# Four-row strips, later turned values, and a last layer with paced loads, finer stores and a 64-row channel product

## The chip, the cores and the metric

The kernel runs on one core of a Trainium2 chip. A core has five engines that run side by side, each with its own instruction queue: TensorE (PE, matrix products, with weight loads listed apart as PEld), VectorE (DVE), ScalarE (ACT), GpSimd (POOL) and SyncE (SP), which only hands out transfers (DMAs). Engines wait for each other through semaphores; an instruction that waits holds up everything behind it in its own queue. Transfers between the large memory (DRAM) and the on-chip memory (SBUF) can be handed out by SP, ACT and POOL. Matrix products land in a small memory, PSUM, from which ACT or DVE copies them to SBUF.

The metric is device microseconds of the launch, as the median of several executions. A further execution is recorded by the profiler; its span runs from the first to the last instruction seen.

## The reference

Input is one image x of 48 channels and 256 x 256 pixels in fp32. Two layers follow, each added to its input, each on a group-normalised input (16 groups of 3 channels, over all pixels).

```
x = x + L0(gn(x));   x = x + L1(gn(x))

L0: qkv = depthwise3x3(w_qkv @ x)            # 144 channels: q, k, v
    cut q, k, v into 4x4 patches, 8 heads     # 66 x 66 patches, border ones are zero; 96 values per patch and head
    q, k scaled to unit length per patch
    attn = softmax(q.T k * temperature)       # per head
    out = v attn, patches put back, then w_proj @ out
L1: windows of 64 x 64 pixels:
    out[C,H,W] = sum over t<3, w, h, c of  x[c,h,w] Ws[t,w,W] Hs[t,h,H] Cs[t,c,C]
```

Within the image there are 4096 patches, so each head has a 4096 x 4096 matrix of logits. The zero border patches are brought in as one extra term of the softmax sum.

## The kernel before

**Stages.** First x is read, its group statistics are formed, and the 1x1 product of heads 0 and 1 is written to the DRAM tensor `t1[0]`. `depthwise_first` then makes q, k and v of head 0 (`qkv[0]` in DRAM). After that the attention loop runs over 8 heads `h` and 16 iterations `g` per head. Then comes the output projection with the second statistics (L783 to L862), and last the window layer (L866 to L1021).

**Attention loop.** One iteration g handles 256 patches of one head as two blocks of 128. Per block TensorE makes the logits (L344) into PSUM tiles `big`, three buffers of two banks, and ACT takes the exponential (L580) with the row sums; DVE scales the value block by them (L598). Then TensorE weighs the values (L614, three pairs per iteration), and DVE adds them up (L628). The order on every engine is the written one (`manual_schedule`). Into this loop is woven the work for the next head: the depthwise convolution of row r = g (loads L209, taps L232 on DVE, `patches`, `high`, `low`, stores L302), the loads of next keys, queries and values (`load_key`, `load_query`, `load_value`, all L318, nearly all from SP), and `turn` (L559), which transposes a value block with TensorE (L562) and copies it to `vT` with ACT (L564). `values[h, m]` is used by iterations g = 2m and 2m+1. `vt`, the block as loaded, has two buffers; `vT` has nine. For head 0, block g+1 is loaded at the top of iteration g (g = 1 to 6) and turned in the same iteration, behind the logits and ahead of the weighing. For later heads two blocks are loaded and turned in each of the iterations 11 to 14 of the head before.

**Strips.** The 1x1 product of heads 2 to 7 is too large to make ahead. It is made in strips of two rows from each half of the image, `class Strip` (L166): `load` brings x (L175, SP, two transfers), `run` makes two products into one `big` tile (L181) and ACT writes them with a bias to an `ot` buffer (L184), `store` writes to `t1[1]` (L193, SP, two transfers). Each iteration has four slots, k = 0 to 3, numbered through by s. Odd slots run two strips and then load the next two; even slots store the two of the slot before. There are 64 strips, so they fill the 64 slots of head 0. `xs` has three buffers of two rows, and `ots` three.

**Last layer.** Units are (yw, xh): one row of windows and half of its columns, 8 in all. `over_c` multiplies by Cs: for each image row one product over the channels (L923), rows of two window halves side by side in the array (partitions 0 to 48 and 64 to 112: 48 channels and a row of ones that carries the mean), into `pa`, three or two rows at a time; DVE or ACT copies it to `lzt` (L935, L933). `over_w` multiplies by Ws (L949) and ACT copies to `lyt` (L956); `over_h` multiplies by Hs (L968) and `residual` adds the input rows `lrt` (L982) and stores from POOL (L989). The opening `over_c(0)` runs alone; after that TensorE's order is, for each of three q of a unit, three times `over_w`, with two groups of the next unit's `over_c` behind each of the first two and `over_h` of the q before behind the third. `begin_load` takes one waiting transfer from a list (rows `lrt`, L884, or pieces `lxq`, L776) and issues it from ACT, where it stands in line with ACT's copies:

```
def begin_load():
    if loads:
        loads.pop(0)()
```

For the first three rows of windows the store waits for both halves and writes 8 channels at full width.

**Between the layers**, `occupy` (L840) puts filler products on TensorE: seven on a constant tile behind the last projection, and one behind each small product of the statistics.

Of the kernel before, what the change touches and what calls it, by code (L numbers as in the profile page):

```python
# [17 lines left out]
C = 48  # L18
# [21 lines left out]
NOT = 3  # L40
# [6 lines left out]
def conv_preact_kernel(  # L47
# [118 lines left out]
    class Strip:  # L166
# [5 lines left out]
        def load(self):  # L172
            self.xs = cv.tile([64 + C, 2, W], F32, name="xs", bufs=3)
            for s, rows in enumerate(both_halves(xc, 2 * self.j, 2)):
                nc.sync.dma_start(out=self.xs[s * 64 : s * 64 + C], in_=rows)  # L175

        def run(self, ps):
            self.ot = ots[self.j % len(ots)]
            for s in range(2):
                r = slice(s * 64, s * 64 + C)  # L180
                nc.tensor.matmul(  # L181
                    ps[:M1, s, :], lhsT=wr[r], rhs=self.xs[r].rearrange("p a b -> p (a b)"), start=True, stop=True
                )
            nc.scalar.activation(  # L184
                self.ot[:, :, 1 : W + 1],
                ps[:M1].rearrange("p s (a b) -> p (s a) b", a=2),
                AF.Identity,
                bias=bias[:M1, 1:2],
            )

        def store(self):
            for s, rows in enumerate(both_halves(t1[1], 2 * self.j, 2, base=1)):
                nc.sync.dma_start(out=rows, in_=self.ot[:, 2 * s : 2 * s + 2, :])  # L193
# [301 lines left out]

    ots = [cv.tile([M1, 4, W + 2], F32, name=f"ot{i}") for i in range(NOT)]
    for t in ots:
        nc.gpsimd.memset(t[:, :, 0:1], 0.0)
        nc.gpsimd.memset(t[:, :, W + 1 : W + 2], 0.0)
    depthwise_first()  # L500

    with tc.If(nc.values_load(large) > 0):
        with tc.tile_pool(name="sps", bufs=2, space=PSUM) as sps:
            for j in range(HALF // 2):
                w = Strip(j)
                w.load()
                w.run(sps.tile([128, 2, 512], F32, name="sps"))
                w.store()
# [27 lines left out]
    with tc.tile_pool(name="ahead", bufs=2) as ah, tc.tile_pool(name="ae", bufs=3) as ae, tc.tile_pool(  # L536
# [3 lines left out]
        NS = 3  # L540
        RP = TP // PX * KS
# [17 lines left out]
        def turn(h, m):  # L559
# [3 lines left out]
            vT = ah.tile([128, 4, HD], F32, name="vT", bufs=9)  # L563
# [89 lines left out]
        strips = [[Strip(s)] if s < HALF // 2 else [] for s in range(NH * NG * NK + 2)]  # L653
        for s in range(2):
            for w in strips[s]:
                w.load()
        with tc.manual_schedule():
            load_query(0, 1)
            block = scores(0, 0)
            for h in range(NH):  # L660
                more = h + 1 < NH
                rows = {r: Depthwise(h + 1, r) for r in range(CR + 1)} if more else {}
                for g in range(NG):
# [7 lines left out]
                    if h == 0 and 0 < g <= 6:  # L671
                        load_value(0, g + 1)
                    if more and CR + 2 <= g < CR + 6:
                        for m in range(2):
                            load_value(h + 1, (g - CR - 2) * 2 + m)
                    if more and CR + 3 <= g < CR + 6:
# [32 lines left out]
                    if h == 0 and 0 < g <= 6:  # L709
                        turn(0, g + 1)  # L710
                    if more and CR + 2 <= g < CR + 6:
                        for m in range(2):
                            turn(h + 1, (g - CR - 2) * 2 + m)
                    if p:
# [7 lines left out]
                    for k in range(NK):  # L722
# [10 lines left out]
                        if s % 2:  # L733
                            for w in strips[s - 1] + strips[s]:
                                w.run(big.tile([128, 2, 512], F32, name="big"))
                            for w in strips[s + 1] + strips[s + 2]:
                                w.load()
                        elif s:
                            for w in strips[s - 2] + strips[s - 1]:
                                w.store()  # L740
# [22 lines left out]
    CK = C + 1  # L763
    units = [(yw, xh) for yw in range(H // WS) for xh in range(2)]
    pieces = [lx.tile([64 + CK, PR, W], F32, name=f"lxq{i}") for i in range(NPC + 1)]
# [12 lines left out]
    with tc.tile_pool(name="pj", bufs=3) as pj, tc.tile_pool(name="pjs", bufs=1) as pjs, tc.tile_pool(  # L778
# [45 lines left out]
        csn = l1c.tile([64 + CK, T3 * C], F32, name="csn")  # L824
# [15 lines left out]
        def occupy(n):  # L840

            for _ in range(n):
                nc.tensor.matmul(busy[:, 0:2, :], lhsT=ident[:, :P2], rhs=nmx, start=True, stop=True)

        with tc.manual_schedule(engines={mybir.EngineType.PE}):
            occupy(7)
            mv1, e1 = group_stats(st1, mean1, rstd1, pjs, pp1, lambda: occupy(1))
            pc1 = pp1.tile([64 + CK, 1], F32, name="pc1", tag="pstat")
            nc.tensor.matmul(pc1, lhsT=gm2, rhs=e1, start=True, stop=True)
            occupy(1)  # L850
# [5 lines left out]
            nc.vector.tensor_scalar_mul(csn, csn, rstd2)  # L856
# [4 lines left out]
            occupy(1)  # L861
            nc.vector.tensor_sub(csn, csn, pb1)  # L862
# [3 lines left out]
    with tc.tile_pool(name="lz", bufs=2) as lz, tc.tile_pool(name="lr", bufs=6) as lr, tc.tile_pool(name="ly", bufs=2) as ly, tc.tile_pool(name="ps1", bufs=2, space=PSUM) as ps1, tc.tile_pool(  # L866
# [22 lines left out]
        loads = []  # L889

        def rows_later(yw, q):

            if yw < H // WS:
                for s in range(2):
                    for c in (0, 4):
                        loads.append(lambda s=s, c=c: load_rows(yw, q, s, c, 4, nc.scalar))

        def piece_later(n):

            yw, i = divmod(n, NPC)  # L900
            if yw < H // WS:
                for s in range(2):
                    for y in range(0, PR, PR // 2):
                        loads.append(lambda s=s, y=y: load_piece(yw, i, s, y, PR // 2, nc.scalar))

        def begin_load():

            if loads:
                loads.pop(0)()

        def over_c(u):
# [4 lines left out]
            for p in range(NPC):  # L916
                xq = piece(yw, p)
                for g, (y0, n) in enumerate(((0, 3), (3, 3), (6, 2))):
                    pa = ps1.tile([128, 2, 512], F32, name="pa")
                    for i in range(n):  # L920
                        for s in range(2):
                            r = slice(s * 64, s * 64 + CK)
# [9 lines left out]
                    if (p * 3 + g) % (4 if u else 2) == 1:  # L932
                        nc.scalar.copy(to, src)  # L933
                    else:
                        nc.vector.tensor_copy(to, src)  # L935
                    if xh and g == 2:
                        piece_later(yw * NPC + p + len(pieces))
                    yield
# [38 lines left out]
        def residual(u, q, pc):  # L977
# [5 lines left out]
            if yw < H // WS - 1:  # L983
                if xh == 0:
                    return
                cols = slice(0, W)
            for s in range(2):
                c0 = s * 24 + q * 8
# [74 lines left out]
```

## Time and profile before

| what | us |
|---|---|
| median of 3 runs | 3606.6 (3599.4 to 3610.64) |
| profiled execution | 3602.95 |
| its span | 3601.1 |
| TensorE busy | 3365.5 (93%) |
| DVE busy | 2026.6 (56%) |
| ACT busy | 1911.9 (53%) |
| POOL busy | 523.9 (15%) |
| first logits of head 0 in a row | from 284.3 |
| last weighing of head 7 | to about 3183 |
| projection and second statistics | to about 3337 |
| last layer | to 3594.5, last store after it |

A row of instructions names line, engine and operation, then out <- in with shapes, the count, busy time and mean duration in ns, and last the idle time before them with what ended it. fp32 matmuls appear as two records each. "A <- B: total, times, longest" is a wait of A that B ended. The granted clock is 1.00 at full speed. In 40 equal slices of the span TensorE is 90% busy or more from slice 17 to slice 35, and less in the slices before, around head 0, and after.

### The profile page before, as it was taken

How to read it: one execution, taken by the hardware profiler on the slowest of the kernel's cores; microseconds unless marked ns; L12 is line 12 of the kernel's file. 1: busy time of each engine (PE TensorE's matmuls, PEld its weight loads, DVE VectorE, ACT ScalarE, POOL GpSimd, SP SyncE). 2: the span in 40 equal slices, each digit the busy share in tenths (PEclk: the TensorE clock that was granted, in tenths of full speed). 3: DMA queues.
4: the chain of work that ended last, by engine and by line, in shares of the span. 5: the costliest groups of instructions: out<-in, count | busy, mean ns of one | idle time of the engine just before them, and what ended most of it. 6: DMA issues, size and time to landing. Idle time of an engine off the chain costs nothing.

```text
span 3601.1 us, 63050 instructions
## 1 busy us (share of the span) xinstructions
PE 3365.5 (93%) x25842; PEld 1871.5 (52%) x25842; DVE 2026.6 (56%) x2983; ACT 1911.9 (53%) x2890; POOL 523.9 (15%) x584
## 2 busy tenths in 40 slices
PE   2878898999999999999999999999999999976898
PEld 1334444555555555555555555555555555532675
DVE  5463665148825882587268727862885222258454
ACT  0245666557655665576456646764666444410443
POOL 2030111012211220122012211221121100010001
PEclk9999999999999999999999999999999999986899
DMA  7455655543332333233333323332233221059664
GB/s 156 165 114 158 156 156 143 166 129 92 87 86 84 97 81 89 83 92 86 82 86 97 91 80 83 94 90 81 80 96 93 64 57 37 19 121 289 140 158 108
DMA packets 240271, 384.10 MB, mean 107 GB/s; under 512 B 77618, under 2 KB 175266, under 8 KB 235464
## 3 DMA queue, kind: packets, MB, share of 16 engines
q1 hardware_dynamic: 187974, 244.77, 24.3%
q0 software_dynamic: 33728, 106.40, 13.1%
q10 hardware_dynamic: 18274, 28.83, 3.6%
q8 instruction: 206, 3.38, 0.4%
q14 instruction: 89, 0.73, 0.1%
HBM read 234.76 MB, written 144.90 MB: 105 GB/s over the span
## 4 chain that ended last, share of the span: by engine, by line
PE 81%; DMA 6%; DVE 2%; issue 1%; ACT 1%; SPq 1%; ACTq 0%; POOL 0%; POOLq 0%; DVEq 0%
PE big L344 38%; PE big L614 36%; PE pc L968 2%; PE pa L923 2%; PE pb L949 2%; DMA t<-ot 1%; PE big L181 1%; DMA pot<-os__70 1%; DMA vt<-qkv 1%; DMA lxq<-x1s 1%; DVE lzt L935 1%; DMA pad<-t 1%; PE pst L562 1%; DVE xt L810 1%; DMA x1s<-pxt 0%
## 5 line engine op out<-in xcount | busy, mean ns | idle before, releaser
L580 ACT ACTIVATE e<-big,nmx 128x1024 f32<-128x1024 f32 x1024 | 1144.3, 1118 | 902.8 <-PE big L344 886.9
L344 PE MATMUL big<-kt,qt 128*128 128x512 f32 x6144 | 1460.2, 395 | 35.1 <-DMA kt<-qkv 26.8
L614 PE MATMUL big<-e,vn 128*32 128x512 f32 x12288 | 1353.7, 595 | 1.0 <-DVE vn L598 1.0
L344 PEld LDWEIGHTS big<-kt,qt 128*128 128x128 f32 x6144 | 1142.6, 189 | 377.4 <-issue 120.1
L628 DVE TENSOR_TENSOR oacc<-big,oacc 128x1024 f32<-128x1024 f32 x359 | 438.6, 1222 | 784.2 <-PE big L614 784.2
L614 PEld LDWEIGHTS big<-e,vn 128*32 128x32 f32 x12288 | 385.2, 110 | 888.3 <-issue 818.1
L232 DVE SCALAR_TENSOR_TENSOR acc<-pad,dwt,acc 126x1024 f32<-126x1024 f32 x592 | 765.6, 1293 | 33.8 <-DMA pad<-t 13.4
L302 POOL DMA_DIRECT2D qkv<-o x72 | 53.1, 737 | 1349.0 <-ACT o L286 1349.0
L296 POOL TENSOR_TENSOR ol<-o,oh 126x1024 fp32r<-126x1024 f32 x78 | 185.2, 2375 | 277.3 <-DVE ss L247 204.4
L594 DVE TENSOR_REDUCE zt<-zs 128x1 f32<-128x5 f32 x256 | 38.7, 151 | 329.8 <-ACT e L580 329.8
L580 ACT ACTIVATION_READ_ACCUMULATOR e<-big,nmx 128x1 f32 x1024 | 196.4, 192 | 0.0
L286 ACT COPY o<-acc 126x1024 f32<-126x1024 f32 x74 | 160.7, 2172 | 0.0
L184 ACT ACTIVATE ot<-big,bias 108x1024 f32<-108x1024 f32 x64 | 68.9, 1112 | 136.7 <-PE big L181 71.0
L935 DVE COPY lzt<-pa 128x864 f32<-128x864 f32 (+1 forms) x69 | 102.1, 1525 | 63.5 <-PE pa L923 63.5
L956 ACT COPY lyt<-pb 128x1024 f32<-128x1024 f32 x69 | 70.9, 1028 | 112.6 <-PE pb L949 106.3
L803 PE MATMUL pps<-pot,wp 96*96 96x512 f32 x128 | 77.8, 773 | 53.3 <-DMA pot<-os__70 40.2
L213 ACT ACTIVATE acc<-pad,dwt 126x1024 f32<-126x1024 f32 x74 | 84.0, 1135 | 73.5 <-DMA pad<-t 73.5
L221 PE MATMUL dps<-pad,diag 126*126 126x512 f32 x216 | 96.4, 606 | 15.0 <-DMA pad<-t 15.0
L243 ACT ACTIVATE sq<-acc 126x1024 f32<-126x1024 f32 x74 | 78.4, 1060 | 59.8 <-DVE acc L232 48.9
L147 ACT ACT_TABLE_LOAD x2 | 2.6, 1283 | 202.6 <-DMA x1s<-pxt 149.2
L247 DVE TENSOR_REDUCE ss<-sq 126x64 f32<-126x1024 f32 x80 | 97.4, 1218 | 6.7 <-ACT sq L243 6.7
L949 PE MATMUL pb<-wsb,lzt 64*64 64x64 f32 x4608 | 88.8, 223 | 11.4 <-issue 7.2
(138 smaller groups left out, 1901.2 us busy)
## 6 DMA issues: line engine op xcount, KB each, us to landing
pad<-t SPq DMA_DIRECT2D x238, 254.0 KB
t<-ot SPq DMA_DIRECT2D x128, 217.7 KB
qkv<-ol POOLq DMA_DIRECT2D x78, 336.0 KB, 6.4
qkv<-oh POOLq DMA_DIRECT2D x70, 336.0 KB, 5.6
qt<-qkv SPq DMA_DIRECT2D x176, 96.0 KB
xs<-in_x_dram SPq DMA_DIRECT2D x128, 96.0 KB
pot<-os__70 SPq DMA_DIRECT2D x16, 768.0 KB
qkv<-o POOLq DMA_DIRECT2D x72, 168.0 KB, 3.4
```

Source lines behind the costliest of these rows:

```text
L213: nc.scalar.mul(self.acc, self.pad[:, 0:KS, 0:W], dwt[:, self.h, 0:1])
L221: nc.tensor.matmul(ps[:, i, :], lhsT=diag[:, tap, :], rhs=self.pad[:, y : y + 2, dx : dx + W], start=(tap == 0), stop=(tap == 8),)
L232: nc.vector.scalar_tensor_tensor(self.acc, self.pad[:, dy : dy + KS, dx : dx + W], dwt[:, self.h, tap : tap + 1], self.acc, ALU.mult, ALU.add,
L247: nc.vector.tensor_reduce(self.ss, self.sq.rearrange("p a (x b) -> p x a b", b=KS), AX.XY, ALU.add)
L286: nc.scalar.copy(self.o.rearrange("p (a b) x -> p a b x", a=KS), self.acc.rearrange("p a (x b) -> p a b x", b=KS))
L296: eng.tensor_sub(self.ol, self.o, self.oh.bitcast(F32))
L344: nc.tensor.matmul(ps[:, i, :], lhsT=qt[:, r, q0 : q0 + 128], rhs=kts[2 * j + i][:, r // 2, :], start=(r == 0), stop=(r == 2),)
L580: nc.scalar.activation(e[:, j * 1024 : (j + 1) * 1024], ps.rearrange("p a b -> p (a b)"), AF.Exp, bias=nmx[:, b : b + 1], accum_out=zs[:, ...
L614: nc.tensor.matmul(ps[p * 32 : (p + 1) * 32, u, :], lhsT=vn[:, c * 32 : (c + 1) * 32], rhs=e[:, n * 512 : (n + 1) * 512], start=(i == 0), ...
L628: nc.vector.tensor_add(oaccs[h, pair], ps, old)
L935: nc.vector.tensor_copy(to, src)
L949: nc.tensor.matmul(pb[s * WS : (s + 1) * WS, w, n * WS : (n + 1) * WS], lhsT=zts[u][r, t * C + b * 24 + q * 8 + s * 4 + i, :], rhs=wsb[r, ...
```

## The change

The edits lie in the attention loop, between the layers and in the last layer.

- **Strips** have four rows (`SR`), so there are 32; each has one load and one store per half. `run` makes two `big` tiles in turn. `xs` and `ots` have two buffers each. An odd slot runs one strip and loads the next; an even slot stores the strip of the slot before.
- **Values.** Head 0's blocks 2 to 7 are loaded at g = 1, 2, 4, 5, 7, 8 (`LOADS`) and each is turned two iterations later. For later heads block 7 is loaded at g = 1 of its own head and turned at g = 2. `vT` has eight buffers.
- **Channel product** over 64 partitions per half (`CF`) instead of 49: the weights of the added rows are zero, the pieces hold ones there.
- **Copies out of `pa`** run over the same elements with rows innermost instead of channels.
- **Loads of the last layer** are issued from SP, each behind a four-byte transfer to a DRAM scratch, `turns`, that reads one element of the tile just copied.
- **Stores of the last layer** come after each half: four of 4 channels and 128 columns.
- **Fillers** ahead of the statistics: two products on rows of the last projected tile and two on the statistics, instead of seven on a constant.

```
-            self.xs = cv.tile([64 + C, 2, W], F32, name="xs", bufs=3)
+            self.xs = cv.tile([64 + C, SR, W], F32, name="xs", bufs=2)
...
+            for i in range(0, SR, 2):
+                ps = pool.tile([128, 2, 512], F32, name="big")
...
-                    if h == 0 and 0 < g <= 6:
-                        load_value(0, g + 1)
+                    if h == 0 and g in LOADS:
+                        load_value(0, 2 + LOADS.index(g))
...
+                    if h > 0 and g == 1:
+                        load_value(h, NM - 1)
...
-                    if h == 0 and 0 < g <= 6:
-                        turn(0, g + 1)
+                    if h == 0 and g - 2 in LOADS:
+                        turn(0, 2 + LOADS.index(g - 2))
...
+                    if h > 0 and g == 2:
+                        turn(h, NM - 1)
...
-                        if s % 2:
-                            for w in strips[s - 1] + strips[s]:
-                                w.run(big.tile([128, 2, 512], F32, name="big"))
-                            for w in strips[s + 1] + strips[s + 2]:
-                                w.load()
+                        if s % 2 and s // 2 < len(strips):
+                            strips[s // 2].run(big)
+                            if s // 2 + 1 < len(strips):
+                                strips[s // 2 + 1].load()
+                        elif s % 2 == 0 and 0 < s // 2 <= len(strips):
+                            strips[s // 2 - 1].store()
...
-            occupy(7)
+            for ki in range(0, KS, 2):
+                occupy(xt[:, ys.start + ki : ys.stop : KS, :])
+            for i in range(0, 4, 2):
+                occupy(st1[:, : HALF * W // 512 - 3 + i, :])
...
-        def begin_load():
-
-            if loads:
+        def begin_load(behind):
+
+            if loads and behind is not None:
+                n = len(taken)
+                taken.append(nc.sync.dma_start(out=turns[:, n : n + 1], in_=behind))
                 loads.pop(0)()
...
-                            r = slice(s * 64, s * 64 + CK)
+                            r = slice(s * 64, s * 64 + CF)
...
+                    copy(to.rearrange("p s y k -> p s k y"), src.rearrange("p s y k -> p s k y"))
...
-                    yield
+                    yield zt[0:1, 0, y : y + 1]
...
-            for s in range(2):
-                c0 = s * 24 + q * 8
-                nc.gpsimd.dma_start(
-                    out=oc[c0 : c0 + 8, yw * WS : (yw + 1) * WS, cols].rearrange("c y x -> y c x"),
+            for c in (0, 4):
+                for s in range(2):
+                    c0 = s * 24 + q * 8 + c
+                    nc.gpsimd.dma_start(
+                        out=oc[c0 : c0 + 4, yw * WS : (yw + 1) * WS, cols].rearrange("c y x -> y c x"),
```

## The prediction

> **What bounds the kernel now.** I read the page's slices and chain first, then compared stretches of one head, then the waits and the chain of the slow head, then the last layer by clock and by shape.
>
> The first answer gives, for each stretch, its length, then busy time and instruction count of PE, PE's weight loads, DVE, ACT and POOL, the granted clock, the DMA share and GB/s. The first two lines are the last layer's opening channel product and the rest of that layer, the third is the head that also runs the strips, the fourth a later head.
>
> ```profile
> 3337.20:3359.30 22.10, 18.39 (x128) 15.62 (x128) 8.72 (x6) 8.71 (x6) 0.00 (x0) 0.50 0.31 57
> 3359.30:3594.50 235.20, 214.71 (x6080) 161.15 (x6080) 126.41 (x90) 100.36 (x90) 19.55 (x28) 0.98 0.60 140
> ...
> 330.80:739.90 409.10, 380.33 (x2316) 196.02 (x2320) 205.61 (x320) 253.19 (x361) 52.58 (x44) 0.95 0.58 156
> 760.00:1109.00 349.00, 349.00 (x2353) 195.74 (x2352) 221.62 (x344) 214.41 (x335) 59.75 (x56) 1.00 0.35 90
> ```
>
> The later heads have no idle TensorE at all, so nothing there can be won except work that is removed, and the change removes none. Head 0 has idle time, and so has the last layer. The chain of head 0, in order of time (start, length, what):
>
> ```profile
> 398.70 12.76 DMA t<-ot
> 411.46 0.02 issue
> 411.48 5.96 DMA vt<-qkv
> 417.44 0.04 issue
> 417.48 0.78 PE pst L562 x4
> 418.27 8.43 PE big L614 x64
> ```
>
> An iteration g that waits for nothing takes 25.74 us in head 0 (weighing starts at 512.12 and 537.86), 25.49 without the norm's matmul, plus 0.33 per turned block. From the weighing of g=1 (330.80) to that of g=15 (739.88) this makes 10 x 25.74 + 4 x 25.49 + 13 x 0.33 = 363.7; it took 409.1. **45 us are stall.** The waits of 330 to 760 us (total, times, longest) name three causes, which add up to 43.7:
>
> ```profile
> ACT ot L184 <- DMA t<-ot: 20.5, 7, 5.2
> ...
> PE pst L562 <- DMA vt<-qkv: 11.6, 5, 4.3
> ...
> PE big L181 <- DMA xs<-in_x_dram: 11.6, 3, 10.8
> ```
>
> All three transfers are handed out by one sequencer, SyncE, and in SyncE's own waits of this window "L175 <- PE big L181" stands with 52.8 us in 19 waits: it sits before a strip load until TensorE has read the buffer, with all later loads behind it.
>
> **The strips.** 64 strips of two rows become 32 of four; matmuls and activations keep number and shape. Loads and stores fall from 128 each to 64 each. At their median issue times (0.422 us for L175, 0.373 for L193) SyncE is spared 64 x 0.795 = 51 us, 3.2 per iteration; bytes are equal. What counts is lead. Before, a strip's buffer is that of three strips ago, whose store is issued one slot (a quarter iteration, 6.4 us) earlier, and the chain shows stores of 8.5 to 12.8 us. After, it is stored three slots (19 us) earlier. I leave 3 of the 20.5 us: **-17.5**; bounds 0 and -20.5. The load after the change goes into a buffer released two slots ago, so SyncE no longer waits at L175; it waits at the next store for the activation instead, about as long, with the query, depthwise and value loads behind it, but the strip's load is already away, three slots before its use instead of two. The worst wait (10.8 us, at 576) came after a three-transfer depthwise load and twelve query transfers had taken 20 us of SyncE; one slot more doesn't hide all of that. Of 11.6 I leave 4: **-7.6**, bounds 0 and -11.6.
>
> **Values turned later.** Loads of head 0 move to g=1, 2, 4, 5, 7, 8, the turns two iterations (51 us) behind, where the chain shows 6 to 8 us per load. **-11.6.** No block is late: m is used from g=2m, and the latest turns are m=2 in 3, m=3 in 4, m=7 in 10. In later heads the last block moves from iteration 14 to g=1 (load) and g=2 (turn) of its own head: the same transposes and transfers, 22 us of weighing and logits as cover. Without that cover it costs 6 to 8 us a head, 50 in all. The turned-value ring of 8 needs no wait: that buffer's last reader is iteration 15. Head 0 together: -36.7 of 45.
>
> **Last layer, the copies out of PSUM.** They now run rows innermost: the destination gets runs of two or three floats instead of single floats 256 B apart, and the source is read in steps of 576 B.
>
> ```profile
> L286 ACT COPY o<-acc 126x1024 f32<-126x1024 f32 x74 | 160.7, 2172 | 0.0
> ...
> L935 DVE COPY lzt<-pa 128x864 f32<-128x864 f32 x46 | 77.4, 1707 | 48.0 <-PE pa L923 48.0
> ...
> L933 ACT COPY lzt<-pa 128x864 f32<-128x864 f32 x18 | 30.0, 1666 | 24.5 <-PE pa L923 20.6 <-DMA lrt<-x1s 2.7 <-DVE lzt L935 1.3
> ...
> L623 DVE COPY oacc<-big 128x1024 f32<-128x1024 f32 x24 | 29.4, 1225 | 94.5 <-PE big L614 94.5
> ...
> L286 ACT COPY o<-dps 126x1024 f32<-126x1024 f32 x6 | 6.1, 1012 | 13.6 <-DVE dps L281 10.3 <-issue 3.3
> ```
>
> Read the mean (second number after the bar). Contiguous, DVE needs 155 ns (its one-element copy L136) plus 1.045 per element, so 864 elements would be 1.06 us; single floats cost 1.71. ACT likewise: 0.88 against 1.67. [...] The two L286 rows say otherwise for ACT: a 16-byte step costs double from SBUF (2172) and nothing from PSUM (1012). I follow the row[...]. DVE about 1.05 to 1.15 us, ACT 0.9 to 1.1. DVE has no row with a PSUM step, so its bounds are 1.06 and, read and write both slow, about 2.0.
>
> **64 rows.** A matmul's time hardly depends on its rows (512 columns: 629 ns in L181 with 48 rows, 595 in L614 with 128), but the clock may. During the opening product, then when L949 has joined:
>
> ```profile
> 3345.00:3350.00 5.00, 4.62 (x36) 3.93 (x36) 1.60 (x1) 2.75 (x2) 0.00 (x0) 0.50 0.09 15
> 3350.00:3355.00 5.00, 4.62 (x36) 3.93 (x36) 2.77 (x2) 1.61 (x1) 0.00 (x0) 0.50 0.01 3
> 3360.00:3365.00 5.00, 5.00 (x140) 4.73 (x132) 1.67 (x1) 1.92 (x2) 0.00 (x0) 0.66 0.41 100
> 3365.00:3370.00 5.00, 3.87 (x159) 3.33 (x148) 2.67 (x2) 2.62 (x3) 0.00 (x0) 1.00 0.90 208
> ```
>
> [...] 92% busy, 0.50 granted for 22 us, while 128-row logits rise 3.7 us after 284.3, and 64-row L949 4 us after 3359.3. [...] by the rows, filled rows count, and the product's 2 x 49 of 128 are what it lacks. I take the second, without certainty. Then some 4.5 us run cold (33 of the 128 matmul records at 137 ns, 24 in 3.28 us) and 95 at the warm 72.5 (24 in 1.74): 11.4, plus waits, 12 for 22.1: **-10**. Staying cold, only the waits for copies go: -3.5. The 0.98 of the rest gains **-2**.
>
> **Rest of the layer.** TensorE idles 20.5 of 235.2 us. Copies 0.6 us shorter, and 88 load issues off ACT (medians 0.604 and 0.309, up to 2.85 in a backlog), take away half: **-10**, bounds 0 and -16. Each load on SyncE has a four-byte transfer before it that waits for a copy: SyncE is otherwise unused here, and 7 pairs per q cost 7 x about 0.9 = 6.3 of 9.1 us.
>
> **Priced at nothing.** Stores 30 to 96: POOL 96 x about 0.6 (estimated from L637's 0.593) against 30 x 0.7 us, idle otherwise. At the end four stores of 128 KB replace two of 256: issues end 1 us later (4 x 0.6 against 2 x 0.7), landing is about 1 us shorter (3.6 median for 256 KB, 2.5 for 192). The filler matmuls fall from 7 to 4 and wait for DVE; the last starts behind the third of the last four statistics (3329.2) and ends before the aggregate does (3331.7); plus or minus 1.
>
> **Sum.** -17.5 -7.6 -11.6 -10 -2 -10 = -58.7. The profiled execution took 3602.95 (span 3601.1): 3544.3; the median of the runs is 3.65 higher: **3548**.
>
> **Rivals.**
> - Clock stays at 0.50 in the opening product (49 rows weren't the reason): 3548 + 6.5 + 2 = 3556. [...]
> - PSUM steps slow DVE: opening -7, rest -3: 3558. For: no DVE row.
> - Head 0 is limited by transfers, not lead: DMA share there is 0.58 against 0.35 later, at a shorter stage it rises to 0.65 (0.58 x 409 / 364). Half of 36.7 comes back as other waits: 3566.
> - Nothing gained: SyncE's new wait at the store delays query loads as much as it spares; about 3606. Against: 51 us fewer issue time.
> - **Slower**: the four-byte transfers read `lyt`, which ACT may not overwrite two q later until they have landed. If SyncE falls behind, TensorE stops. At the worst issue seen, 2.85 + 0.4 us for each of 7 pairs, a q takes 22.8 instead of 9.1; 88 loads fill 12.6 such q: +172, 3720. It outweighs the 58.7 from 13.8 us per q, 1.97 us per pair. Against: medians of half that.
>
> **Chances.** Forecast 0.42 (own range 3535 to 3562), cold clock 0.20, slow copies 0.13, transfers 0.16, nothing 0.04, slower 0.05. The range 3529 to 3582 holds the first four with their bounds. A difference under 0.3% can't be told from none: faster 0.90, same 0.04, slower 0.06.
>
> **What would show it.** Waits on `t<-ot`, `vt` and `xs` in head 0 at a few us; iterations of 26 us. L935 near 1.1 us, L933 near 1.0. Granted clock 1.0 within 5 us of the opening product. No wait of ACT L956 for a transfer. I am wrong if head 0 keeps over 20 us of stall, if L935 stays at 1.7, or if ACT waits for SyncE's small transfers.

## The result, and the profile after

The changed kernel takes 3553.4 us (median of 4 runs, 3547.5 to 3561.6) against 3603.0 for the kernel before beside it (4 runs, 3597.9 to 3610.6). The ratio is 0.9862, 95% interval 0.9834 to 0.989: **faster by about 50 us**. The forecast was 3548, with a range of 3529 to 3582. Measured again, the same kernel gave 0.9896 (0.9878 to 0.9914). The profiled execution of after took 3547.5 us, its span is 3545.7, so the profiled pair differs by 55.4 us.

First the stretches of the changed kernel, in the columns of the prediction's first fence (busy time and count of PE, weight loads, DVE, ACT, POOL; granted clock, DMA share, GB/s): opening channel product, rest of the last layer, head 0 (here from 325.0 to 701.6; the two weighings that bound it elsewhere begin at 330.3 and 706.3), a later head.

```profile
3307.80:3321.40 13.60, 10.30 (x132) 8.43 (x132) 5.92 (x6) 5.35 (x6) 0.00 (x0) 1.00 0.50 94
3321.40:3537.80 216.40, 206.54 (x6080) 158.06 (x6080) 94.58 (x90) 89.07 (x90) 57.58 (x92) 1.00 0.63 153
325.00:701.60 376.60, 370.70 (x2316) 194.27 (x2315) 208.86 (x323) 256.19 (x361) 52.54 (x44) 0.99 0.63 170
760.00:1109.00 349.00, 349.00 (x2352) 196.37 (x2348) 221.19 (x344) 215.39 (x336) 59.72 (x56) 1.00 0.34 87
```

Head 0 from the weighing of g=1 to that of g=15 went from 409.1 to 376.0, the opening product from 22.1 to 13.6, the rest from 235.1 to 216.4. The later heads are as they were. Cut at the same marks in both traces, the difference is -33.1 (head 0), +0.4 (later heads), +3.7 (projection and statistics, 142.6 to 146.2), -8.6 (opening), -18.7 (rest), +1.3 (behind the last residual), and -0.4 before g=1: together -55.4. (Before, the last weighing of head 7 ends at 3194.7, not at about 3183 as the table of the kernel before has it; and by the page's slices TensorE is 90% busy or more from slice 8 on, not 17.)

What waits in head 0 now (325 to 720 us; total, times, longest):

```profile
PE big L184 <- DMA xs<-in_x_dram: 5.9, 4, 3.8
PEld big L184 <- DMA xs<-in_x_dram: 3.3, 2, 3.1
```

And the longest of SyncE's own waits in the same window:

```profile
SPq L200 <- ACT ot L191: 57.8, 14, 9.1
```

Waits for `t<-ot` (20.5 us before) and for `vt` (11.6) are gone. SyncE waits about as long as it did (52.8 before), but now at the store (L200) and no longer at the strip's load. What is left sits almost wholly in one iteration of 36.3 us (g=4); all others take 25.5 to 26.9. Of its 10 us over an iteration without waits, TensorE is idle for 5.4; behind that the granted clock is 0.50 for 10.2 us. SyncE's sequencer there (start, length, instruction, count):

```profile
400.90 2.19 SPq L176 DMA_DIRECT2D xs<-in_x_dram  x2
403.13 0.89 SPq L325 DMA_DIRECT2D vt<-qkv  x2
404.12 12.47 SPq L325 DMA_DIRECT2D qt<-qkv  x12
416.69 0.91 SPq L200 DMA_DIRECT2D t<-ot  x2
417.64 2.86 SPq L176 DMA_DIRECT2D xs<-in_x_dram  x2
```

The strip's load at 417.64 stands behind twelve query transfers (12.47 us) and a store.

In the last layer, the copies by shape (second number behind the bar: mean ns), and then two slices of the opening product:

```profile
L951 DVE COPY lzt<-pa 128x864 f32<-128x864 f32 x46 | 51.2, 1125 | 44.7 <-PE pa L941 44.7
...
L951 ACT COPY lzt<-pa 128x864 f32<-128x864 f32 x18 | 18.6, 1032 | 15.1 <-PE pa L941 15.0
```

The slices, in the columns of the first fence:

```profile
3310.00:3315.00 5.00, 3.53 (x42) 2.74 (x44) 1.91 (x2) 2.67 (x3) 0.00 (x0) 1.00 1.03 196
3315.00:3320.00 5.00, 4.34 (x58) 3.68 (x60) 2.10 (x3) 2.04 (x3) 0.00 (x0) 1.00 0.31 53
```

DVE's three-row copy fell from 1707 to 1125 ns, ACT's from 1666 to 1032. The clock, 0.50 all through this product before, is 1.00.

Last, the longest waits of TensorE in the rest of the layer, in the kernel before:

```profile
PE pb L949 <- issue: 7.2, 8, 2.2
PE pa L923 <- ACT lzt L933: 2.6, 2, 2.0
PE pa L923 <- DVE lzt L935: 2.5, 6, 0.4
```

The same view of after:

```profile
PE pb L965 <- issue: 3.5, 5, 1.1
PE pc L984 <- issue: 1.8, 4, 0.8
PE pb L965 <- ACT lyt L972: 1.6, 3, 1.1
```

Waits for the copies of `pa` are gone, and "issue", for which the page names no releaser, is the largest one in both kernels. It became the question of the experiments.

### The profile page after: what moved, and what is told of

Its sections match the earlier page's. It is cut to its first block, busy times and chain, and to the rows that moved or that the text cites. A ratio compares the mean times of both kernels' runs of the same rounds, so it can differ in the third digit from the quotient of the medians.

```text
span 3545.7 us, 63152 instructions
## 1 busy us (share of the span) xinstructions
PE 3339.1 (94%) x25836; PEld 1859.1 (52%) x25836; DVE 1990.7 (56%) x2983; ACT 1900.0 (54%) x2890; POOL 562.6 (16%) x648
## 5 line engine op out<-in xcount | busy, mean ns | idle before, releaser
L351 PE MATMUL big<-kt,qt 128*128 128x512 f32 x6144 | 1457.3, 394 | 31.2 <-DMA kt<-qkv 26.2
L325 POOL DMA_DIRECT2D kt<-qkv x44 | 23.0, 543 | 516.5 <-PE big L351 504.3
L951 DVE COPY lzt<-pa 128x864 f32<-128x864 f32 (+1 forms) x69 | 67.4, 1000 | 59.7 <-PE pa L941 59.7
```

Source lines behind the costliest of these rows:

```text
L351: nc.tensor.matmul(ps[:, i, :], lhsT=qt[:, r, q0 : q0 + 128], rhs=kts[2 * j + i][:, r // 2, :], start=(r == 0), stop=(r == 2),)
```

## The experiments

All times are ratios or medians against the kernel before on the same chip (3595.5 beside the first eight runs, 3593.7 beside the last four). Stages are those of the profiled execution of each. "Idle" is TensorE's idle time within the rest of the last layer, and in head 0.

| kernel | head 0 (idle) | opening (clock) | rest (idle) | span |
|---|---|---|---|---|
| before | 409.1 (28.8) | 22.1 (0.50) | 235.1 (20.4) | 3601.1 |
| values alone | 396.6 (21.9) | 22.1 (0.50) | 246.0 (26.0) | 3602.3 |
| values, four buffers | 390.2 (9.4) | 22.1 (0.50) | 233.8 (22.3) | 3584.1 |
| 64 rows alone | 394.5 (18.6) | 17.7 (0.91) | 239.4 (26.2) | 3591.4 |
| copy order alone | 404.0 (20.1) | 19.1 (0.50) | 234.4 (20.7) | 3599.1 |
| after | 376.0 (5.9) | 13.6 (1.00) | 216.4 (9.8) | 3545.7 |
| after, once more | 385.4 (10.5) | 15.7 (0.78) | 218.7 (11.4) | 3565.1 |
| after, old value turns | 394.0 (18.8) | 14.1 (0.92) | 218.3 (12.1) | 3565.1 |
| after, 49 rows | 382.0 (9.9) | 15.7 (0.89) | 220.1 (11.9) | 3559.0 |
| after, old copy order | 378.9 (7.8) | 18.4 (0.84) | 222.2 (14.2) | 3558.9 |
| after, loads on ACT | 372.9 (4.0) | 14.0 (0.91) | 227.4 (17.8) | 3557.2 |
| after, no turns | 381.1 (10.2) | 16.2 (0.74) | 241.6 (26.6) | 3584.5 |
| after, late loads left out | 381.6 (9.3) | 14.2 (0.90) | 209.2 (6.6) | 3542.3 |
| after, strips loaded earlier | 364.1 (0.0) | 14.5 (0.87) | 218.3 (11.6) | 3540.7 |

The table says how far one profile can be trusted. Three kernels have the head 0 of before untouched: 409.1, 394.5, 404.0. Seven have that of after: 372.9 to 385.4. So a difference of under some 15 us in head 0 between two single profiles shows nothing. The opening scatters by up to 2.6 us among like kernels. The rest scatters by 2.3 us among the four kernels that have that of after (after twice, old value turns, strips loaded earlier), but by 12 among the three that have that of before (before, and both kernels with the values: 233.8 to 246.0).

**Head 0: strips without the values.** Here the load and turn times of head 0's values were undone in the changed kernel; the eight `vT` buffers stay.

```
-                    if h == 0 and g in LOADS:
-                        load_value(0, 2 + LOADS.index(g))
+                    if h == 0 and 0 < g <= 6:
+                        load_value(0, g + 1)
...
-                    if h == 0 and g - 2 in LOADS:
-                        turn(0, 2 + LOADS.index(g - 2))
+                    if h == 0 and 0 < g <= 6:
+                        turn(0, g + 1)
```

> The changed kernel with head 0's values loaded and turned in the same iteration again. Theory (each of the three waits has its own price): the waits for the value loads come back at about their old 11.6 us, so the stretch of head 0 from the weighing of g=1 to that of g=15 is 387 to 390 us instead of 376, and the whole about 3565. Rival (the value loads were late only because the strip stores filled SyncE's queue): with the long strips these waits stay under 4 us, the stretch under 380, the whole at 3553 to 3557.

Measured: 3577.4 us, ratio 0.9954 (0.9938 to 0.997); head 0 394.0. The waits for `ot` are gone and those for `xs` down to 1.0, but TensorE waits 19.9 us for `vt`, where it waited 11.6 before. Neither number was met. The likely reading is that part of what the strips give back goes to the next late transfer while the values are turned in the iteration that loads them. On top of the strips, then, the later turns are worth some 14 us of head 0 (394.0 against 379.7 in the mean of the seven).

**Values without the strips**, on the kernel before: the load and turn edits of the change, and eight `vT` buffers.

```
-                    if h == 0 and 0 < g <= 6:
-                        turn(0, g + 1)
+                    if h == 0 and g - 2 in LOADS:
+                        turn(0, 2 + LOADS.index(g - 2))
...
+                    if h > 0 and g == 2:
+                        turn(h, NM - 1)
```

> The kernel before with the values alone loaded earlier and turned later. Theory: 11.6 us go and the waits for strip buffers and strip loads stay: stretch of head 0 397 to 400 us instead of 409, the whole about 3591. Rival (one backlog, whose delay moves on to the next user): the other two waits grow by what this one loses, stretch 405 to 409, the whole within 3 us of before.

Measured: 3592.0 us, ratio 0.9991 (0.9978 to 1.0004); head 0 396.6. Its waits in head 0:

```profile
ACT ot L184 <- DMA t<-ot: 19.9, 6, 8.0
PE big L181 <- DMA xs<-in_x_dram: 18.7, 4, 10.6
```

The mirror image: no wait for `vt`, and the wait for `xs` up from 11.6 to 18.7. In the time no gain can be measured. The two parts seem to be worth more together than one by one (6 us for the values and 8.5 for the strips, single profiles against the mean of before's three; 23 for both); that this is because both wait on one queue fits the waits, but the sizes lie near the scatter.

**Lead without fewer transfers**: the values again, and the two-row strips of before with four buffers of `xs` and of `ot`, which hold as many rows as after's two of four.

```
-NOT = 3
+NOT = 4
...
-            self.xs = cv.tile([64 + C, 2, W], F32, name="xs", bufs=3)
+            self.xs = cv.tile([64 + C, 2, W], F32, name="xs", bufs=4)
```

> The kernel before with the values as in the change, and two-row strips with four buffers each of xs and ot, the same memory as the change's two buffers of four rows. Lead as after the change, 256 strip transfers as before it. Theory (lead): stretch of head 0 376 to 382 us, as with the change, the whole about 3570. Rival (number of transfers: 51 us of SyncE's issue time): stretch 390 to 398, the whole about 3588.

Measured: 3586.3 us, ratio 0.9973 (0.9958 to 0.9987); head 0 390.2. The same view:

```profile
PE big L181 <- DMA xs<-in_x_dram: 9.4, 7, 3.8
ACT ot L184 <- DMA t<-ot: 9.0, 2, 6.8
PEld big L181 <- DMA xs<-in_x_dram: 7.2, 5, 2.2
```

More buffers halve both waits and do not end them; 390.2 is in the rival's range. The same buffer space with half the transfers leaves 5.9 and 10.5 us of `xs` on PE in the two profiles of after, none of `ot`, and a head of 379.7 in the mean of the seven. Of the way from 396.6 to there, 6 us go with the buffers and some 10 with the fewer transfers; both are inside the scatter of single profiles, so the split is not firm.

**Opening product: 49 rows** in the changed kernel.

```
-    CF = 64
+    CF = CK
```

> The changed kernel with 49 rows in the channel product again. Theory (filled rows keep the clock up): granted clock 0.5 in most of the opening product, which takes 18 to 20 us instead of 13.6. Rival (the new fillers keep the clock up until it begins, and from there 49 rows are enough): clock 1.0 and 13 to 15 us.

Measured: 3560.8 us (one run); opening 15.7. The product starts at clock 1.00, falls to 0.50 for 3.4 us after a lull in which TensorE waited for copies, and comes back with 49 rows, after TensorE was 100% busy in these 3.4 us. So 49 rows do not hold the clock down in every case.

**64 rows alone**, on the kernel before, with its copies, loads and fillers:

```
+    CF = 64
...
-                            r = slice(s * 64, s * 64 + CK)
+                            r = slice(s * 64, s * 64 + CF)
```

> The kernel before with the channel product over 64 rows and nothing else changed. Theory (filled rows let the clock rise): the clock is released about 5 us into the opening product, which takes 15 to 17 us instead of 22.1. Rival (TensorE comes to it out of a lull, and the gaps that slow copies leave keep it down): 0.50 throughout and 22 us as in the three runs with 49 rows and slow copies.

Measured: 3593.2 us (one run); opening 17.7. A slice ahead of the product, which starts at 3327.7, and two within it:

```profile
3325.00:3327.60 2.60, 1.88 (x4) 0.84 (x4) 0.85 (x4) 0.05 (x1) 0.00 (x0) 0.50 0.03 13
3330.00:3335.00 5.00, 3.49 (x41) 2.71 (x38) 2.33 (x2) 2.31 (x2) 0.00 (x0) 0.91 1.06 178
3335.00:3340.00 5.00, 3.32 (x40) 2.67 (x40) 3.23 (x2) 3.04 (x3) 0.00 (x0) 1.00 0.00 0
```

The time is just above the 15 to 17 us expected. From a cold start full clock comes 3.2 us into the product, in which TensorE was never idle, and it stays with TensorE 66 to 70% busy. In the other kernels with 64 rows that begin cold it comes after 2.2 to 3.8 us, but in "after, no turns" only after 8.5.

**Copy order alone**, on the kernel before (ACT's copy is changed alike):

```
-                        nc.vector.tensor_copy(to, src)
+                        nc.vector.tensor_copy(to.rearrange("p s y k -> p s k y"), src.rearrange("p s y k -> p s k y"))
```

> The kernel before with the row-innermost copies out of PSUM alone. Both theories: L935 about 1.0 us instead of 1.53 on the mean of both shapes, L933 about 0.92 instead of 1.56. Theory rows: the clock stays at 0.50 in the opening, 18 to 19 us. Rival (gaps): without waits for copies TensorE is never idle, the clock rises after 4 to 5 us, 14 to 16 us. The rest of the layer: 222 to 226 us instead of 235 if copies are half of its gain, 217 if they are all of it, 232 if the loads on ACT are nearly all.

Measured: 3592.2 us, ratio 0.9985 (0.9969 to 1.0); opening 19.1, rest 234.4. Two slices of its opening product:

```profile
3345.00:3350.00 5.00, 4.74 (x40) 4.39 (x38) 1.12 (x1) 1.53 (x2) 0.00 (x0) 0.50 0.16 28
3350.00:3355.00 5.00, 4.80 (x38) 4.39 (x38) 1.81 (x2) 1.15 (x1) 0.00 (x0) 0.50 0.01 3
```

These two runs are the clearest pair. Both products start cold and do the same matmuls but for the rows; with 49 rows and TensorE 89% busy (95% in these slices) the clock stays at 0.50 to the end, with 64 rows it is released. But before its release TensorE was 100% busy, so the pair alone leaves busy time as a rival.

The traces settle more of this. In all fourteen profiles the granted clock changes in steps of 3.41 us, and for each step TensorE's busy share can be counted (worked out from the records, in which the ends of matmuls are modelled). At 0.50, ten steps filled by 49-row channel products, 92 to 97% busy, were all followed by 0.50; one that was 100% busy, in the changed kernel with 49 rows, was followed by full clock. With 64 rows, steps of 87, 92, 97 and 100% were followed by full clock, and two of 77 and 78% were not. So the rows count here and the filled time too. Losing the clock is another matter: all 155 full-clock steps under 40% busy were followed by 0.50, and none of some 13,000 over 80%. This is no complete rule, since of 194 cold steps of other matmuls with TensorE 100% busy 25 were followed by 0.50. But by these counts 66 to 70% keeps a clock that 92% with 49 rows doesn't bring back, and an idle stretch can cost TensorE more than its own length: 5.4 us idle in g=4 of after, and 0.50 for 10.2 us behind them.

The shorter copies, alone, gave the rest of the layer no gain that stands out from the scatter (234.4; 233.8 to 246.0 without them). TensorE's waits for copies of `pa` fell from 5.1 us to 1.6, but "issue" stood at 12.2 (9.4 before). The ratio leaves room for 0 to 11 us in the whole kernel, 3 of them in the opening.

**Old copy order in the changed kernel**, the other way round:

```
-                    copy(to.rearrange("p s y k -> p s k y"), src.rearrange("p s y k -> p s k y"))
+                    copy(to, src)
```

> The changed kernel with the old order of the copies out of PSUM (channels innermost), all else as changed. If the shorter copies are worth something once the loads have left ACT: rest of the last layer 225 us or more (216.4 in the changed kernel), opening 16 to 18 us (13.6), because DVE again needs 1.5 to 1.7 us a copy. Rival, that the copies gave the rest nothing here either, as they gave nothing alone in the kernel before: rest 215 to 220, opening 14 to 16.

Measured: 3560.7 us (one run); rest 222.2, between the two expectations; opening 18.4, just above the first. By this single profile the copies are worth about 4 us in each stage once the loads are paced; DVE's copy is back at 1710 ns. In the opening part of it is the clock, which fell again for 3.4 us.

**Loads on ACT, without turns**, in the changed kernel (the pieces' loads alike):

```
-                        loads.append(lambda s=s, c=c: load_rows(yw, q, s, c, 4, nc.sync))
+                        loads.append(lambda s=s, c=c: load_rows(yw, q, s, c, 4, nc.scalar))
...
-                taken.append(nc.sync.dma_start(out=turns[:, n : n + 1], in_=behind))
+                taken.append(None)
```

> The changed kernel with the last layer's loads issued from ACT again, without the four-byte transfers. Theory (half of the gain of the rest of the layer is the loads' place): rest 222 to 227 us instead of 216.4 to 220.1, with ACT's L972 later. Rival (all of it is the faster copies): 216 to 220.

Measured: 3555.6 us, ratio 0.9887 (0.9856 to 0.9919); rest 227.4, of which 17.8 idle. "Issue" is 13.0 us of that, against 5.3 in after; the waits for ACT's `lyt` are as short (1.9 and 1.6), so ACT is hardly later. The profile has 9 to 11 us more in this stage than after; the times do not confirm it, since after has 0.9862 and 0.9896.

**Loads on SyncE, without turns**, only the last line of that diff:

> The changed kernel with the loads on SyncE but without the four-byte transfers ahead of them, so that SyncE issues each load as soon as its buffer is free. Theory (the pace doesn't matter, since ACT is spared either way): rest of the layer 215 to 220 us, as with the change. Rival (loads in a heap crowd the first row loads, the weights and the stores): rest 222 us or more, with waits for lrt.

Measured: 3575.5 us, ratio 0.9943 (0.9922 to 0.9965); rest 241.6, worse than before. TensorE's waits in this stage:

```profile
PE pb L965 <- issue: 18.7, 11, 4.3
PE pc L984 <- issue: 3.6, 3, 3.1
```

Neither ACT nor DVE is late in it; of the idle time nothing but "issue" has grown, from 5.3 to 22.3 us. The same matmuls also take 8.5 us more, at a mean clock of 0.96 instead of 1.00. So, for loads on SyncE, the four-byte transfer is the part that matters: without it SyncE sends the loads as soon as their buffers are free, up to 28 in a row (16 pieces from 3337.2 and 12 of `lrt` from 3361.4). What TensorE waits for can be looked for among the DMA packets. The trace has a queue of 16 KB packets of kind "instruction", 48 of them in this stage, one per 5 us, or about 250 of TensorE's 12,160 matmul and weight-load records to each. The longest gaps of TensorE in this run beside the packet nearest to each (worked out from the trace's records; us):

```
gap from   long   to        packet from   to        gap's end after packet's
3367.19    3.11   3370.30   3367.34       3368.64   1.66
3380.86    2.23   3383.09   3380.33       3381.65   1.44
3434.04    3.11   3437.15   3434.71       3435.79   1.35
3443.36    1.92   3445.28   3442.67       3444.00   1.27
3499.26    4.28   3503.54   3500.89       3501.90   1.65
```

Of the 14 gaps over 0.5 us in this run, the waits name a releaser for two, an ACT and a DVE instruction. The other 12 all end 1.0 to 1.7 us after such a packet has landed, though packets come only every 5 us. The same holds for all 36 gaps without a releaser in six further traces (six each in before, after, after once more and strips loaded earlier, ten with the loads on ACT, two without the late loads): 1.2 to 1.8 us. By chance it would be about one in six. In three of the five the packet itself started only when TensorE was idle already.

**The late loads left out.** If the gaps come from the loads' traffic, they go when the loads go:

```
-                for s in range(2):
-                    for c in (0, 4):
-                        loads.append(lambda s=s, c=c: load_rows(yw, q, s, c, 4, nc.sync))
+                rts[yw, q] = lr.tile([128, 8, W], F32, name="lrt")
+                nc.gpsimd.memset(rts[yw, q], 0.0)
...
-                        loads.append(lambda s=s, y=y: load_piece(yw, i, s, y, PR // 2, nc.sync))
+                        loads.append(lambda: None)
```

> The changed kernel without the last layer's late loads: the residual's rows are set to zero by GpSimd, and pieces 33 and up keep the rows that their buffers held, so this part of the output isn't the reference's; the four-byte transfers of the pieces' turns stay. Theory: TensorE's idle time put down to issue (5.6 us in the changed kernel, 22.3 without turns) is the wait for the next 16 KB of its own instructions[...]. Then it falls below 2 us here and the rest of the layer is 209 to 213 us (206.6 of work in the changed kernel, plus the waits at its end). Rival, that the gaps are TensorE's own: issue stays at 5 to 6 us, the rest at 214 to 217.

Measured: 3544.1 us (one run); rest 209.2. TensorE's waits there:

```profile
PE pb L964 <- issue: 2.3, 2, 1.4
PE pb L964 <- ACT lyt L971: 1.6, 3, 1.1
```

It held in the main: 2.3 us of "issue" where below 2 was expected, against the rival's 5 to 6 and 5.3 to 7.6 in the kernels with paced loads; the rest is in the range. That these gaps come with the loads is what this one profile shows (2.3 us without the late loads, 5.3 with them). That TensorE waits for what the instruction packets bring was not shown; it rests on their times alone (each gap over 0.5 us without a named releaser ends 1.0 to 1.8 us after a packet). Whatever holds TensorE up there, it takes 22.3 us of 241.6 with unpaced loads and 5.3 of 216.4 with paced ones.

**After, once more**, as the measure for the last run:

> The changed kernel once more, as the measure for the next run on the same chip: 3546 to 3562 us, ratio to the kernel before 0.983 to 0.989.

Measured: 3558.8 us (4 runs, 3554.2 to 3566.9), ratio 0.9896 (0.9878 to 0.9914): just outside the expected ratio. Its profiled execution was the longest of the four, with head 0 at 385.4, and here the clock fell to 0.50 for 6.8 us, 1 us into the opening product, with 64 rows. That the first profile shows 1.00 throughout is not the rule.

**Strips loaded earlier.** Two strips are loaded ahead of the loop, and each later one in the even slot, ahead of the store: one slot earlier than after (the text on record says two), and not behind the store's wait. The last four stores are shared by three queues.

```
         strips[0].load()
+        strips[1].load()
...
-                            if s // 2 + 1 < len(strips):
-                                strips[s // 2 + 1].load()
                         elif s % 2 == 0 and 0 < s // 2 <= len(strips):
+                            if s // 2 + 1 < len(strips):
+                                strips[s // 2 + 1].load()
                             strips[s // 2 - 1].store()
...
+            engs = (nc.sync, nc.scalar, nc.gpsimd, nc.sync) if (u, q) == (NU - 1, NQ - 1) else (nc.gpsimd,) * 4
```

> The changed kernel with two differences: strips 0 and 1 are loaded ahead of the loop and strip j+1 later in an even slot, ahead of the store in SyncE's queue (so at least two slots more of lead, and no load behind a store's wait); and the four stores of the very last residual are shared by SyncE, ACT and GpSimd. If what is left of the stall in head 0 (5.9 us of idle TensorE, one iteration of 36.3 us) is the strip's load standing late in SyncE's queue: stretch of head 0 366 to 370 us (376.0 in the changed kernel), tail 6 to 7 us (7.9), total 5 to 10 us under the changed kernel on the same chip. Rival, that the transfers themselves are what is late (the queries and values beside them): stretch 373 to 377, total within 3 us.

Measured: **3541.8 us** (4 runs, 3540.4 to 3549.9), ratio 0.9858 (0.9838 to 0.9879): 17 us under after once more by the medians (the two intervals just touch; 5 to 10 us were expected), and the lowest median of all. The profiles account for it: 15.6 us in head 0 against the mean of after's, 1.9 behind the last residual. Head 0 in the columns of the first fence:

```profile
331.40:695.50 364.10, 364.10 (x2316) 190.99 (x2316) 205.61 (x321) 254.94 (x360) 52.55 (x44) 1.00 0.64 175
```

Head 0 has no idle TensorE left, at the same bytes in less time (DMA share 0.64), and the granted clock is 1.00; 364.1 is what the prediction had worked out for a head without stall (363.7). The rival, that the transfers limit it, fell. The stretch behind the last residual is 6.0 us, 7.9 in after.

## Why the prediction was right or wrong, point by point

The direction, the size and the places were right: 3553 against 3548, in head 0, the opening product and the rest. That the sum came so close is in part luck, since terms that missed offset each other. Against means over like kernels (three with each untouched stage of before, four to seven with that of after), head 0 gained 23 us (402.5 to 379.7), the opening 7.5 (22.1 to 14.6), the rest 20 (238.3 to 217.9, the first a mean of values 12 apart).

- **Base of head 0 (45 us of stall): an unlucky profile, and its parts misread.** Among the three kernels with that head, the profiled execution of before had the most stall; their mean is 38.8 (402.5 less 363.7). And of the 45 us TensorE was idle for 28.8 only. The other 16.6 are its own work at a lower clock: 380.3 us busy at 0.95 before, 364.1 at 1.00 with strips loaded earlier, for the same matmuls. The 43.7 us of the three waits matched the 45 by chance, because they take a wait of ACT for one of TensorE and leave out the clock. What of ACT's 20.5 us for `t<-ot` reached TensorE, in the kernel before:

```profile
PE big L344 <- ACT ot L184: 5.8, 3, 2.5
```

  The -36.7 of the sum were 33.1 in the pair of profiles and 23 in the means. Of these 23, 14 are idle time (22.5 to 8.2 us in the means) and the rest is clock.
- **Strips, `ot` (-17.5): right in kind, too large as a wait of TensorE.** The wait is gone in the kernels with four-row strips, but for one of 4.7 us with strips loaded earlier, which left TensorE no idle time. It had cost TensorE 5.8 us directly.
- **Strips, `xs` (-7.6): size off, by a miscount.** The working said that the load is away three slots before its use instead of two. The code issues it in the odd slot before, two slots ahead, as before; only the wait in front of it went. 5.9 and 10.5 us were left in the two profiles of after, where 4 were predicted. The earlier load supplied the missing slot, and head 0 had no stall.
- **"What counts is lead": half wrong.** Four buffers without fewer transfers took 6 us off head 0, inside the scatter, and left 18.4 us of waits on `xs` and `ot`. The place in SyncE's queue counts, as the strips loaded earlier show (364.1 us of head 0 against 379.7 in the mean), and by the waits the number of transfers in front of a load too; the 51 us of spared issue time were worked out and then given no term.
- **Values (-11.6): right as a wait, not a term of its own.** The wait went, and alone it bought no time that can be measured, since another wait on the same queue grew by 7 us; together with the strips it was worth some 14 us. The later heads lost nothing, as priced: 2455.3 against 2454.9.
- **Copies: durations right** (1125 and 1032 ns, forecast 1.05 to 1.15 and 0.9 to 1.1; for DVE, with no row of a PSUM step before, that was the author's estimate), so PSUM steps of 576 B cost DVE 0.07 us and ACT 0.15 at most, measured against the prediction's 1.06 and 0.88 for contiguous copies, and that rival is out.
- **64 rows (-10): mis-sized**, 8.6 in the pair and 7.5 in the means. The prediction put the cold clock down to the rows, because 92% busy had not ended it. That set busy time aside too soon: in the changed kernel 49 rows came back to full clock after a step of 100%. The rows count beside it, since 87% was enough with 64 rows and 97% was not with 49. And 64 rows fell from full clock in two kernels (after once more, and after with the old copy order), behind steps 58 and 49% busy. What else the clock goes by stays open.
- **Clock of the rest (-2): mis-sized, 8.** TensorE's busy time there fell from 214.7 to 206.6 us at the same number of instructions, and it was 211.4 to 220.0 in the three kernels with the rest of before.
- **Rest of the layer (-10): right size, cause right in part.** Idle time fell from 20.4 to 9.8. The working gave it to shorter copies and to ACT's spared issues. Of the 10.6 us, 5.1 are waits for the copies of `pa`, as predicted; 4.1 are "issue", which the working did not have; the waits for ACT's `lyt` fell by only 0.8. Copies alone gave nothing that can be told from the scatter. Taking the loads off ACT without pacing left 15 to 17 us more idle time than after, so on SyncE the pacing is needed, done by the very transfers that the prediction looked at only as a risk. Against loads on ACT it gains 9 to 11 us in one profile and nothing in the times, so what pacing is worth there stays open. The slower rival did not come up. ACT waited for one of the transfers once:

```profile
ACT lyt L972 <- DMA turns<-lzt: 2.5, 1, 2.5
```

- **Priced at nothing.** The end behind the last residual cost 1.3 us. The projection and statistics are 3.7 longer in the pair, but the kernels before range from 142.6 to 148.6 and those after from 145.9 to 154.1, so the small fillers can't be told from nothing. The fillers and the finer stores were not run by themselves.

## What to carry to other kernels

Where several late transfers share one queue, mending one wait can move the time to the next (here `vt`'s 11.6 us went and the wait for `xs` grew from 11.6 to 18.7); count what stands in front of each load in the queue, slot by slot in the code, and put a load ahead of anything that waits (in head 0 that took TensorE's idle time from 5.9 us to none). A stall can cost more than its idle time, because the clock falls behind it (16.6 of the 45 us in head 0 before were the same matmuls taking longer at a mean clock of 0.95): compare TensorE's busy time for the same matmuls too, and don't count another engine's wait as TensorE's. A wait for which the profile names no releaser is worth a look at the DMA packets of the instructions: loads from SyncE that go out one by one can be faster than loads that go out as early as possible (216.4 against 241.6 us in the rest of the last layer). And before a stall is priced from one profile, its scatter should be known: here it was 15 us in one head of the same code.

## What was not expected of the hardware

- TensorE's gaps without a named releaser all end 1.0 to 1.8 us after a 16 KB instruction packet has landed (48 gaps over 0.5 us, seven traces of the last layer); with unpaced loads on SyncE the "issue" waits of one stage rose from 5.3 to 22.3 us, and without the late loads they fell to 2.3.
- A product that kept TensorE 89% busy with 49 rows per half ran at a granted clock of 0.50 for all its 19.1 us (copy order alone), while with 64 rows, also begun cold, full clock came after 2.2 to 3.8 us in six kernels and after 8.5 in a seventh (after, no turns).
- At a granted clock of 0.50, ten steps of 3.41 us that were 92 to 97% busy with 49 rows did not bring full clock back, and a step of 87% with 64 rows did; at 1.00, none of some 13,000 steps over 80% busy lost it, and all 155 under 40% did.
